# A graph attention block on one core: a fourth raw weight buffer, weights requested a slot sooner, and some steps put in another order

## The chip, the core and the metric

The kernel runs on one core of one Trainium2 chip. The metric is the device time of one execution in microseconds; for each kernel the median of several runs is given. The engines are called as in the profile: PE (matrix products; PEld is its weight load), DVE (vector), ACT (activations), POOL (GpSimd) and SP (the queue that issues most DMAs). Each engine works off its own queue in program order, and waits on semaphores for what other engines or DMAs must have done.

## What is computed

384 nodes with 1024 features, 6528 edges of five types, 16 heads of 64 features. All values are float32.

```python
h = relu(layernorm(x))                      # 384 x 1024
q, k, v = h @ wq.T + bq, h @ wk.T + bk, h @ wv.T + bv
q2, k2, v2 = q @ wiq.T + biq, k @ wik.T + bik, v @ wiv.T + biv      # then split in 16 heads
mask[src, dst] = softplus(edge_type_weights)[edge_type - 1]         # -inf where there is no edge
attn = softmax(q2 @ k2.T / 8 + mask)        # per head, 384 x 384
return x + (attn @ v2) @ wo.T + bo
```

When an edge occurs several times, the last one counts; the diagonal gets the fourth weight where no edge gives it one.

## The kernel before

To keep float32 accuracy on a product type that rounds its inputs, each operand is split in a high and a low half (`hi` is the rounded value, `lo` the rest), and each product is made three times: hi by hi, hi by lo, lo by hi (`mm3`, L366; lines L367, L368 and L369).

The seven weight matrices come as 56 chunks of 128x1024 (L51 to L55), in the order v, q, iv, k, then iq and ik in turn, then o. `load(w)` (L60) requests chunk w on SP into one of the `raw` buffers; `split_hi(w)` (L67) rounds it on ACT (L77), `split_lo(w)` (L79) subtracts on DVE or POOL (L82). The halves lie in four `whl` buffers. A chunk of a projection takes one "slot" of 24 products over 384 tokens. `slot_head(w)` (L395) opens a slot: it splits chunk w+2, evacuates the previous slot's bank, and calls load(w+4).

**Start** (L93 to L124, L311 to L363). SP requests the three tiles of x; between the first and the second stands the request of the edge rows `er` (L98). Then come chunk 0, the edges `ed`, chunk 1 and small constants. `key_rows` (L180) makes on POOL, in L182 to L184, a key of each edge from `er` and writes it to DRAM (`krow`); `key_load` (L196) reads it back, spread over all partitions, into `rows`. Then, for each x tile, DVE takes the statistics (L251, L254), ACT and POOL subtract the mean (L280, L282; DVE does so for tile 2), PE transposes (L292), `ln_hi` (L298) makes the high half on ACT and `ln_lo` (L303) the low one on DVE. POOL also splits chunk 0 (L344, L346), turns the edges into floats (L150) and makes the low half of chunk 1 (L82). `warm(n)` gives PE n idle transposes. The first chunk's 24 products (L410 to L415) have an order of their own: all eight hi by hi, then the others in groups of four.

**Projections.** Beside them, DVE looks for double edges (`mask_detect`, L217) in `rows`, and POOL scatters the mask values (L228) into three DRAM tables, which table_clear (L146) fills first from a tile `zero`. `evac_row` (L380) evacuates a bank through a tile of the tag `e` (L382, then ACT L383). The tiles `er`, `zero`, `kr` (the keys) and `lnt` (the statistics) have the tag `e` too, and that tag has EB buffers, used in turn.

**Attention** (L685 on). 48 steps (16 heads by three row tiles) run as a hand-written pipeline, L767 on. In round i: scores of step i on PE (`do_S`, L694, two products, two score banks); for i-1 `do_ttr` on DVE (L700: adds the mask, finds the extreme, writes an `e` tile and so frees the score bank); for i-2 the exponential on ACT (L704); for i-3 the normalisation (L708 on DVE, L709 on POOL); for i-5 the transposes on PE (`do_T`, L714); for i-6 their split (L723 on ACT, L724 on DVE); every third round the product with v2 (L731) and its evacuation (L741, L742, L746, L747). `fill(n)` puts other products between: first those of iq and ik (`fill_qk`, with `qk_head`, L576; `qk_done`, L548, evacuates with L377 and L378 and sends the halves through DMAs L557 to L567 to the stacks that the scores read), then those of the output matrix (`fill_o`, L657). `wo_prep` (L623) splits an output chunk and calls load(WO+k+2); OPOOL names the output chunks whose low half POOL makes.

**Output.** The output is summed in two halves of four chunks. After the fourth chunk `ysum` (L651, DVE's L654) adds the bank to the residual tile, and the bank becomes free for the next tile.

Of the kernel before, what the change touches and what calls it, by code (L numbers as in the profile page):

```python
# [8 lines left out]
F32 = mybir.dt.float32  # L9
# [5 lines left out]
N, D, NT, KT, NP = 384, 1024, 3, 8, 8  # L15
# [7 lines left out]
def gnn_kernel(ctx: ExitStack, tc: tile.TileContext, x, edges, erows, etw, wq, wk, wv, wiq, wik, wiv, wo,  # L23
# [6 lines left out]
    nc = tc.nc  # L30
    const = ctx.enter_context(tc.tile_pool(name="const", bufs=1))
    big = ctx.enter_context(tc.tile_pool(name="big", bufs=1))
    wpool = ctx.enter_context(tc.tile_pool(name="wpool", bufs=4))
# [2 lines left out]
    dram = ctx.enter_context(tc.tile_pool(name="dram", bufs=1, space=bass.MemoryType.DRAM))  # L36
    ctx.enter_context(tc.manual_schedule())

    EB = 8
    NTAB, RNG = 3, EC // 3  # L40
    JI = [0, 1, 3, 5, 8, 11, 14, RNG]
    WARM = (20, 6, 0)
# [1 line left out]
    def bank(tag):  # L44
        return psum.tile([128, 512], F32, tag=tag, name=tag, bufs={"g": 3, "a": 1}.get(tag, 2))
# [11 lines left out]
    raw, whl = {}, {}  # L57
    NCH = len(chunks)

    def load(w):  # L60
        if w >= NCH:
            return
        n, m = chunks[w]
        raw[w] = wpool.tile([128, D], F32, tag="raw", name="raw", bufs=3)
        nc.sync.dma_start(raw[w], W[n][m])

    def split_hi(w, dst=None, dve=False):  # L67
# [26 lines left out]
    er = ert[:, :2 * EC].bitcast(I32)  # L94
    for t in range(NT):
        nc.sync.dma_start(xt[t], x[t * 128:(t + 1) * 128, :])
        if t == 0:
            nc.sync.dma_start(er, erows)  # L98
    load(0)
    ed = const.tile([128, 3 * EC], I32, name="ed")  # L100
    nc.sync.dma_start(ed, edges)
# [78 lines left out]
    def key_rows():  # L180

        nc.gpsimd.tensor_copy(kf, er)  # L182
        nc.gpsimd.tensor_scalar(kf[:, :EC], kf[:, :EC], float(N), None, op0=OP.mult)
        nc.gpsimd.tensor_tensor(krt[:, :EC], kf[:, :EC], kf[:, EC:], OP.add)  # L184
        nc.sync.dma_start(krow.rearrange("c j -> (c j)").rearrange("(p e) -> p e", p=128), krt[:, :EC])
# [10 lines left out]
    def key_load(g, s):  # L196

        if s == 0:
            t = work.tile([128, 2, NT, N], F32R, tag="pt", name="rows")
            krv[g] = t.bitcast(F32).rearrange("p a k n -> p (a k n)")  # L200
        c0, c1 = parts(g)[s]
        dst = krv[g][:, s * PA * 128:(s * PA + c1 - c0) * 128]
        for c in range(c0, c1):
            rows[c] = krv[g][:, (s * PA + c - c0) * 128:(s * PA + c - c0 + 1) * 128]
        nc.sync.dma_start(dst, krow[c0:c1, :].rearrange("c j -> (c j)").partition_broadcast(128))
# [44 lines left out]
    def ln_bn(t, h):  # L250
        nc.vector.bn_stats(lnt[:, 30 + 12 * t + 6 * h:36 + 12 * t + 6 * h], xt[t][:, h * 512:(h + 1) * 512])  # L251
# [25 lines left out]
    def ln_sub(t, c0, c1, eng):  # L277
        src, dst = xt[t][:, c0:c1], xn[t][:, c0:c1]
        if eng is nc.scalar:
            nc.scalar.activation(dst, src, AF.Identity, bias=negm[:, t:t + 1])  # L280
        elif eng is nc.gpsimd:
            nc.gpsimd.tensor_tensor(dst, src, lnt[:, 2 * t:2 * t + 1].to_broadcast([128, c1 - c0]), OP.subtract)  # L282
        else:
            nc.vector.tensor_scalar(dst, src, lnt[:, 2 * t:2 * t + 1], None, op0=OP.subtract)
# [11 lines left out]
    def ln_hi(t, half, ps):  # L296
        hi = hT[:, 0, half * 4:half * 4 + 4, t * 128:(t + 1) * 128]
        nc.scalar.activation(hi, ps.rearrange("p (k n) -> p k n", k=4), AF.Relu)  # L298
# [11 lines left out]

    mask_consts()  # L311
    warm(WARM[0])
    key_rows()
    load(2)
    for s in range(NTAB):
        key_load(0, s)
    ln_bn(0, 0)
    ln_bn(0, 1)
    ln_mean(0)
# [1 line left out]
    ln_sub(0, 512, D, nc.gpsimd)  # L321
    p0 = ln_transpose(0)
    warm(WARM[1])
    ln_hi(0, 0, p0[0])
    ln_hi(0, 1, p0[1])
    ln_bn(1, 0)
    ln_bn(1, 1)
    ln_mean(1)
    ln_sub(1, 0, 512, nc.scalar)
    ln_sub(1, 512, D, nc.gpsimd)  # L330
    ln_bn(2, 0)
    ln_bn(2, 1)
    ln_mean(2)
# [10 lines left out]
        nc.gpsimd.tensor_copy(t0[:, 0, c], raw[0][:, c])  # L344
    for c in (slice(0, 512), slice(512, D)):
        nc.gpsimd.tensor_tensor(t0[:, 1, c], raw[0][:, c], t0[:, 0, c].bitcast(F32), OP.subtract)  # L346
    load(3)
    ln_hi(2, 0, p2[0])
    ln_hi(2, 1, p2[1])
    ln_root()  # L350
# [35 lines left out]
    w = 0  # L386
# [8 lines left out]
    def slot_head(w):  # L395
        if w > 0:
            split_hi(w + 2)
        if w != 1:
            flush()
        split_lo(w + 2)  # L400
        while post:
            post.pop(0)()
        load(w + 4)

    def proj(src, dst, bidx, extra=None):
        nonlocal w
        for m in range(8):
            slot_head(w)
            ps = bank("g")
            if w == 0:  # L410
                for a, b, ks in ((0, 0, range(KT)), (1, 0, range(4)), (0, 1, range(4)), (1, 0, range(4, KT)),
                                 (0, 1, range(4, KT))):
                    for k in ks:
                        nc.tensor.matmul(ps[:, :N], whl[0][a][:, k * 128:(k + 1) * 128], src[:, b, k, :],  # L414
                                         start=(a == b == k == 0), stop=(b == 1 and k == KT - 1))  # L415
            else:
                for k in range(KT):
                    colmm(ps, w, src, k)
                    if w == 1 and k == 3:
                        ln_row()  # L420
                        flush()
            pend.append(lambda ps=ps, m=m: evac_row(ps, dst[:, 0, m, :], dst[:, 1, m, :],
                                                bc[:, bidx * 8 + m:bidx * 8 + m + 1]))
            if extra:
                extra(m)
            w += 1
# [149 lines left out]
    def qk_head(w):  # L576
        first = w - W0 < 3
        if not first:
            load(w + 4)
            split_hi(w + 2)  # L580
        if pendq:
            pendq.pop(0)()
        if 0 < w - W0 < NTAB:
            mask_select(w - W0)
        if first:
            split_hi(w + 2)
        split_lo(w + 2, nc.gpsimd if (w + 2) % 2 == PAR else None)
        if first:
            load(w + 4)
        if w == W0:  # L590
            mask_select(0)

# [18 lines left out]
    WO = NCH - 8  # L611
# [1 line left out]
    LT, LA = 5, 7  # L613
    PRE, RATE, RATE_O, RATE_E = 84, 7.9, 8, 8
    WSTEPS = (37, 40, 42, 44, 47, 51)
    PAR, OPOOL, ODVE = 1, (2, 3, 6), (2,)

    otile = {}
    oacc = {}
# [3 lines left out]
    def wo_prep(k):  # L623

        dst = None
        if k == 4:
            otile[0] = gtile("g3").rearrange("p a k n -> p (a k n)")
        if 4 <= k < 7:
            g, b = otile[0], (k - 4) * 2048
            dst = (g[:, b:b + 1024], g[:, b + 1024:b + 2048])  # L630
        split(WO + k, nc.gpsimd if k in OPOOL else None, dst, k in ODVE)
        load(WO + k + 2)

    def xb_load():

# [15 lines left out]
    def ysum(a, c=(0, 512)):  # L651
        t, h = OT[a]
        y = xb[t][:, h * 512 + c[0]:h * 512 + c[1]]
        nc.vector.tensor_tensor(y, oacc[t, h][:, c[0]:c[1]], y, OP.add)  # L654
        return y

    def fill_o():  # L657


        first = [(0, 0), (0, 1), (1, 0), (1, 1), (2, 0), (2, 1)]  # L660
        first += [(a, k) for k in (2, 3) for a in range(3)] + [(a, k) for a in range(3, 6) for k in range(KH)]
        for a, k in first:
            while now[0] < wready[k] or now[0] < 6 * k + OREADY or (k == KH - 1 and now[0] < XSTEP + 3):
                yield 0
            if k == 0:
                oacc[OT[a]] = bank("g")
            omm(*OT[a], k)
            if k == KH - 1:
                ysum(a)
            yield 4  # L670
        bank_step = (0, 0, 0, 49, 50)
        todo = [(a, k) for k in range(KH, 7) for a in range(5)]
        while todo:
            ready = [q for q in todo if now[0] >= max(6 * q[1] + OREADY, wready[q[1]], bank_step[q[0]])]
            if not ready:
                yield 0
                continue
            a, k = ready[0]
            todo.remove(ready[0])
            if k == KH:  # L680
                oacc[OT[a]] = bank("gggss"[a])
            omm(*OT[a], k)
            yield 4
# [83 lines left out]
    for i in range(S + LA + 4):  # L767
        now[0] = i
        r = RATE if len(gens) == 2 else RATE_O if i < S else RATE_E
        fill(r / 2)  # L770
        if i < S:
            do_S(i)
        fill(r / 2)
        if 0 <= i - 1 < S:
            do_ttr(i - 1)
        if 0 <= i - 2 < S:
            do_exp(i - 2)
        if 0 <= i - 3 < S:
            do_norm(i - 3)
        if 0 <= i - LT < S:  # L780
            do_T(i - LT)
        j = i - LA
        if j >= 2 and (j - 2) % 3 == 0 and (j - 2) // 3 < 16:
            do_A((j - 2) // 3)
        if 0 <= i - LT - 1 < S:
            do_pt(i - LT - 1)
        if j >= 3 and (j - 3) % 3 == 0 and (j - 3) // 3 < 16:
            do_ao((j - 3) // 3)
        if j >= 4 and (j - 4) % 6 == 3:
            do_aos((j - 4) // 3)  # L790
        run_tasks()
        if i == XSTEP:
            assert len(gens) < 2
            xb_load()
        if i in WSTEPS:
            wo_prep(wp)
            wready[wp] = i + 2
            wp += 1
# [57 lines left out]
```

## Time and profile before

| | |
|---|---|
| runs: median (lowest to highest) | 302.63 us (301.64 to 302.9), 3 runs |
| the profiled execution | 302.19 us, span of its trace 300.5 us |
| granted clock of PE | 0.999 of full speed |
| busy share of the span: DVE, ACT, POOL | 67%, 52%, 52% |
| bytes moved | 55.12 MB, 183 GB/s over the span |
| first real product (L414) starts | 12.26 us |
| last step of the attention pipeline on DVE (L742) starts | 287.14 us |

The profile is one execution. Its page lists the busy time of the engines, the chain of work that ended last (followed back from the last instruction, at each step to what released it), and groups of instructions by line. The timeline lists instructions in order: start in us, duration in us, engine, line, operation, output<-input, shapes, count; in square brackets the engine's idle time before it and what ended it. PE's products overlap, so their durations are longer than their spacing: what counts is the distance from start to start.

The stretches of the run, with the busy time of each engine (and the number of instructions):

```profile
core 0: us, PE busy (x) PEld busy (x) DVE busy (x) ACT busy (x) POOL busy (x), PEclk, DMA share, GB/s
0.00:12.26 12.26, 8.71 (x51) 6.86 (x51) 6.55 (x14) 6.16 (x12) 7.25 (x19) 1.00 0.79 270
12.26:111.00 98.74, 98.74 (x527) 93.19 (x528) 70.08 (x191) 41.23 (x52) 60.42 (x66) 1.00 0.65 216
...
160.00:250.00 90.00, 89.93 (x545) 87.42 (x544) 59.27 (x173) 63.62 (x148) 48.86 (x47) 1.00 0.67 166
250.00:275.00 25.00, 24.77 (x134) 21.02 (x133) 19.24 (x55) 17.53 (x41) 18.20 (x16) 1.00 0.53 179
275.00:300.50 25.50, 21.98 (x117) 18.76 (x115) 10.55 (x18) 5.40 (x11) 4.12 (x5) 0.99 0.17 62
```

### The profile page before, as it was taken

The page shows a single profiled execution, that of the slowest core. Times are in us where ns is not written, and L with a number is a line of the kernel's source. Part 1 is how long each engine was busy: PE and PEld are TensorE (multiplying, and loading weights), DVE is VectorE, ACT ScalarE, POOL GpSimd, SP SyncE. Part 2 cuts the span into 40 slices and gives each one's busy share as a digit, 9 for nine tenths or more (in the row PEclk, how much of TensorE's full clock was granted, in tenths as well). Part 3 has the DMA queues.
Part 4 walks back from the last instruction along what each step waited for, and adds up shares of the span by engine and source line. Part 5 has one row for each costly group of instructions (what it writes and reads, how often), then busy time and mean ns, then how long its engine had stood idle before and what let it go on. Part 6 is the DMA issues. An engine that isn't in the chain of part 4 may idle for free.

```text
span 300.5 us, 4961 instructions
## 1 busy us (share of the span) xinstructions
PE 293.1 (98%) x1649; PEld 276.1 (92%) x1649; DVE 200.5 (67%) x492; ACT 154.9 (52%) x289; POOL 155.7 (52%) x164
## 2 busy tenths in 40 slices
PE   7899999999999999999999999999999999999995
PEld 5699999999988889999999999999999998888884
DVE  2959986655956463788865576767576757696523
ACT  3874644333422213554325667777777767676310
POOL 5865766271555785730033737373746467566210
PEclk9999999999999999999999999999999999999999
DMA  7899754642686668475369997646565636910005
GB/s 233 284 297 381 281 164 171 228 143 70 217 238 224 193 217 242 142 274 198 115 169 244 217 221 173 166 127 180 155 170 139 174 81 174 381 41 0 2 0 209
DMA packets 22377, 55.12 MB, mean 183 GB/s; under 512 B 4816, under 2 KB 8400, under 8 KB 22352
## 3 DMA queue, kind: packets, MB, share of 16 engines
q1 hardware_dynamic: 19968, 52.42, 57.7%
q0 software_dynamic: 2064, 1.80, 2.0%
q10 hardware_dynamic: 320, 0.59, 0.8%
q8 instruction: 13, 0.21, 0.3%
q14 instruction: 12, 0.10, 0.1%
HBM read 40.39 MB, written 4.97 MB: 151 GB/s over the span
## 4 chain that ended last, share of the span: by engine, by line
PE 95%; DMA 2%; DVE 1%; ACT 0%; issue 0%; SPq 0%
PE g L369 21%; PE g L367 21%; PE g L368 21%; PE s L694 6%; PE a L731 6%; PE t L714 5%; PE s L369 2%; PE s L368 2%; PE s L367 2%; DMA g<-in_x_dram 2%; PE t L369 2%; PE t L367 2%; PE t L368 2%; PE g L414 1%; PE a L369 1%; PE a L367 1%
## 5 line engine op out<-in xcount | busy, mean ns | idle before, releaser
L367 PE MATMUL g<-g,whl 128*128 128x384 f32 x312 | 106.4, 341 | 0.0
L369 PE MATMUL g<-g,whl 128*128 128x384 f32 x312 | 104.5, 335 | 0.0
L368 PE MATMUL g<-g,whl 128*128 128x384 f32 x312 | 104.2, 334 | 0.0
L228 POOL DMA_INDIRECT tab<-val,idx x51 | 57.6, 1129 | 40.3 <-issue 11.3
L77 ACT ACTIVATE whl<-raw 128x1024 fp32r<-128x1024 f32 x51 | 53.4, 1051 | 31.7 <-PE g L369 20.1
L709 POOL TENSOR_TENSOR e<-e,s 128x384 f32<-128x384 f32 x48 | 39.2, 830 | 41.2 <-DVE s L708 32.9
L368 PEld LDWEIGHTS g<-g,whl 128*128 128x128 f32 x312 | 58.7, 188 | 0.0
L367 PEld LDWEIGHTS g<-g,whl 128*128 128x128 f32 x312 | 58.6, 188 | 0.0
L369 PEld LDWEIGHTS g<-g,whl 128*128 128x128 f32 x312 | 58.5, 188 | 0.0
L82 DVE TENSOR_TENSOR whl<-raw,whl 128x1024 fp32r<-128x1024 f32 x41 | 50.2, 1224 | 9.6 <-ACT whl L77 7.9
L82 POOL TENSOR_TENSOR whl<-raw,whl 128x1024 fp32r<-128x1024 f32 x11 | 26.5, 2412 | 35.6 <-ACT whl L77 31.8
L383 ACT ACTIVATE g<-f,bc 128x384 fp32r<-128x384 f32 x24 | 14.8, 618 | 53.1 <-DVE f L382 46.8
L704 ACT ACTIVATE e<-e,s 128x384 f32<-128x384 f32 x48 | 29.4, 612 | 13.0 <-DVE s L700 13.0
L724 DVE TENSOR_TENSOR pt<-t,pt 128x384 fp32r<-128x384 f32 x48 | 26.4, 550 | 13.9 <-ACT pt L723 13.3
L723 ACT ACTIVATE pt<-t 128x384 fp32r<-128x384 f32 x48 | 23.2, 484 | 13.9 <-PE t L714 13.3
L700 DVE CUSTOM_DVE_ANT_0 e<-s,ma 128x384 f32<-128x384 f32 x48 | 26.3, 550 | 2.0 <-PE s L694 1.8
L694 PE MATMUL s<-ks,qs 128*128 128x384 f32 x96 | 25.3, 344 | 0.3 <-DVE s L700 0.2
L714 PE MATMUL t<-ident,e 128*128 128x128 f32 x144 | 23.5, 271 | 0.0
L382 DVE TENSOR_TENSOR f<-g,rrow 128x384 f32<-128x384 f32 x24 | 13.3, 555 | 13.5 <-PE g L369 7.6
L714 PEld LDWEIGHTS t<-ident,e 128*128 128x128 f32 x144 | 18.8, 140 | 3.1
L378 DVE SCALAR_TENSOR_TENSOR nat<-g,bc,nat 128x384 fp32r<-128x384 f32 x16 | 9.9, 618 | 16.4 <-ACT nat L377 14.4
L731 PE MATMUL a<-pt,vhl 128*128 128x384 f32 x96 | 20.8, 351 | 0.0
(147 smaller groups left out, 414.8 us busy)
## 6 DMA issues: line engine op xcount, KB each, us to landing
ks<-nat SPq DMA_DIRECT2D x30, 192.0 KB
raw<-in_wv_dram SPq DMA_DIRECT2D x8, 512.0 KB
raw<-in_wq_dram SPq DMA_DIRECT2D x8, 512.0 KB
raw<-in_wiv_dram SPq DMA_DIRECT2D x8, 512.0 KB
raw<-in_wk_dram SPq DMA_DIRECT2D x8, 512.0 KB
raw<-in_wiq_dram SPq DMA_DIRECT2D x8, 512.0 KB
raw<-in_wik_dram SPq DMA_DIRECT2D x8, 512.0 KB
raw<-in_wo_dram SPq DMA_DIRECT2D x8, 512.0 KB
```

The source lines that it names most:

```text
L77: nc.scalar.activation(dst[0], raw[w], AF.Copy)
L82: (eng or nc.vector).tensor_tensor(lo, raw[w], hi.bitcast(F32), OP.subtract)
L228: nc.gpsimd.indirect_dma_start(out=tabs[c // RNG], out_offset=bass.IndirectOffsetOnAxis(ap=idx[:, c:c + 1], axis=0), in_=val[:, c:c + 1], ...
L367: nc.tensor.matmul(ps, lhi, rhi, start=first, stop=False)
L368: nc.tensor.matmul(ps, lhi, rlo, start=False, stop=False)
L369: nc.tensor.matmul(ps, llo, rhi, start=False, stop=last)
L694: nc.tensor.matmul(ps[:, :N], qs[:, o, t * 128:(t + 1) * 128], ks[:, o, s, :], start=(s == 0), stop=(s == 1))
L704: nc.scalar.activation(es[i], es[i], AF.Exp, bias=s[:, 0:1], scale=-1.0, accum_out=s[:, 1:2])
L709: nc.gpsimd.tensor_tensor(es[i], es[i], s[:, 2:3].to_broadcast([128, N]), OP.mult)
L714: nc.tensor.transpose(ps[:, k * 128:(k + 1) * 128], es[i][:, k * 128:(k + 1) * 128], ident)
L724: nc.vector.tensor_tensor(lo, pv, hi.bitcast(F32), OP.subtract)
L731: nc.tensor.matmul(ps[:, :N], vhl[:, k, p, 2 * o:2 * o + 2, :], pts[h][:, s, k, :], start=(k == 0 and s == 0), stop=(k == 2 and s == 1))
```

## The change

- `raw` has four buffers instead of three, and every call of load asks for one chunk further: load(w+5) for load(w+4), load(WO+k+3) for load(WO+k+2). At the start load(3) stands beside load(2), and load(4) where load(3) was.
- The tag `e` has six buffers instead of eight.
- The edge rows are requested behind the third x tile instead of behind the first.
- `key_rows`, load(2) and the first `key_load`s stand behind the mean subtraction of x tile 1. On POOL the key rows so come after the second L282 instead of ahead of the first. The `ln_hi` of tile 0 stand behind the subtraction of tile 1 on ACT.
- The eight hi by hi products of chunk 0 are made for tokens 0 to 255 first and then for tokens 256 to 383, as sixteen. The others are as before.
- A sum of the output half (`ysum`) is put in a list. The list is worked off after the next `do_ttr`, or ahead of the next use of a bank.
- OPOOL gets chunk 4: its low half goes from DVE to POOL.

In the built order of instructions PE's queue differs in the sixteen products alone; DVE's in round 42 (the low half of output chunk 4 is gone, L700 stands ahead of two L654 instead of behind them); ACT's and POOL's in what is named above.

```diff
-    EB = 8
+    EB = 6
...
-        raw[w] = wpool.tile([128, D], F32, tag="raw", name="raw", bufs=3)
+        raw[w] = wpool.tile([128, D], F32, tag="raw", name="raw", bufs=4)
...
         nc.sync.dma_start(xt[t], x[t * 128:(t + 1) * 128, :])
-        if t == 0:
-            nc.sync.dma_start(er, erows)
+    nc.sync.dma_start(er, erows)
...
     warm(WARM[0])
-    key_rows()
-    load(2)
-    for s in range(NTAB):
-        key_load(0, s)
     ln_bn(0, 0)
...
     warm(WARM[1])
-    ln_hi(0, 0, p0[0])
-    ln_hi(0, 1, p0[1])
     ln_bn(1, 0)
     ln_bn(1, 1)
     ln_mean(1)
     ln_sub(1, 0, 512, nc.scalar)
     ln_sub(1, 512, D, nc.gpsimd)
+    ln_hi(0, 0, p0[0])
+    ln_hi(0, 1, p0[1])
+    key_rows()
+    load(2)
+    load(3)
+    for s in range(NTAB):
+        key_load(0, s)
...
-    load(3)
+    load(4)
...
-        load(w + 4)
+        load(w + 5)
...
-                for a, b, ks in ((0, 0, range(KT)), (1, 0, range(4)), (0, 1, range(4)), (1, 0, range(4, KT)),
-                                 (0, 1, range(4, KT))):
+                al = (0, N)
+                for a, b, ks, (n0, n1) in ((0, 0, range(KT), (0, 256)), (0, 0, range(KT), (256, N)),
+                                           (1, 0, range(4), al), (0, 1, range(4), al), (1, 0, range(4, KT), al),
+                                           (0, 1, range(4, KT), al)):
...
-            load(w + 4)
+            load(w + 5)
...
-    PAR, OPOOL, ODVE = 1, (2, 3, 6), (2,)
+    PAR, OPOOL, ODVE = 1, (2, 3, 4, 6), (2,)
...
-        load(WO + k + 2)
+        load(WO + k + 3)
...
+    ysums = []
+
+    def flush_y():
+        while ysums:
+            ysum(ysums.pop(0))
...
             if k == 0:
+                flush_y()
                 oacc[OT[a]] = bank("g")
             omm(*OT[a], k)
             if k == KH - 1:
-                ysum(a)
+                ysums.append(a)
...
             do_ttr(i - 1)
+        flush_y()
```

More of the change, by code (lines that the diff above doesn't have):

```diff
@@ L410, in proj @@
             if w == 0:
-                for a, b, ks in ((0, 0, range(KT)), (1, 0, range(4)), (0, 1, range(4)), (1, 0, range(4, KT)),
-                                 (0, 1, range(4, KT))):
+                al = (0, N)
+                for a, b, ks, (n0, n1) in ((0, 0, range(KT), (0, 256)), (0, 0, range(KT), (256, N)),
+                                           (1, 0, range(4), al), (0, 1, range(4), al), (1, 0, range(4, KT), al),
+                                           (0, 1, range(4, KT), al)):
                     for k in ks:
-                        nc.tensor.matmul(ps[:, :N], whl[0][a][:, k * 128:(k + 1) * 128], src[:, b, k, :],
-                                         start=(a == b == k == 0), stop=(b == 1 and k == KT - 1))
+                        nc.tensor.matmul(ps[:, n0:n1], whl[0][a][:, k * 128:(k + 1) * 128], src[:, b, k, n0:n1],
+                                         start=(a == b == k == n0 == 0), stop=(b == 1 and k == KT - 1))
             else:
@@ L588, in qk_head @@
         if first:
-            load(w + 4)
+            load(w + 5)
         if w == W0:
@@ L775, in gnn_kernel @@
             do_ttr(i - 1)
+        flush_y()
         if 0 <= i - 2 < S:
```

## The prediction

> **What bounds the kernel now.** I read the page first (parts 1 and 4), then the chain in order of time for the start, then timelines of the few places where the matrix engine stands still. The page says that there is little to win:
>
> ```profile
> PE 293.1 (98%) x1649; PEld 276.1 (92%) x1649; DVE 200.5 (67%) x492; ACT 154.9 (52%) x289; POOL 155.7 (52%) x164
> PE 95%; DMA 2%; DVE 1%; ACT 0%; issue 0%; SPq 0%
> ```
>
> 95% of the chain that ended last is matrix products. A matrix product over 384 columns starts every 0.173 us, one over 512 every 0.227, and from 12.26 to 160 us PE is busy without a gap. What is not products lies in three places: the first 12.26 us, a few waits of L694 between 160 and 270, and the 3.5 us after the last product (297.0 to 300.5), which no edit touches. The start, by the chain in order of time:
>
> ```profile
> 1.72 5.41 DMA g<-in_x_dram
> 7.16 1.30 DVE lnt L251 x2
> ...
> 11.51 0.66 PE a L292 x4
> 12.17 0.09 issue
> ```
>
> The second x tile (landed 7.13) sets everything up to the first product. But POOL has a chain of its own beside it:
>
> ```profile
> 4.35 0.27 POOL L182 CAST er<-er 128x102 f32<-128x102 int32 x1 [1.77 <-DMA er<-in_erows_dram]
> ...
> 5.20 0.29 POOL L184 TENSOR_TENSOR kr<-er 128x51 f32<-128x51 f32 x1
> ...
> 8.77 1.04 POOL L282 TENSOR_TENSOR g<-g,lnt 128x512 f32<-128x512 f32 x1 [1.96 <-DVE lnt L254]
> 9.81 1.36 POOL L344 CAST whl<-raw 128x512 fp32r<-128x512 f32 x2
> 11.14 2.72 POOL L346 TENSOR_TENSOR whl<-raw,whl 128x512 fp32r<-128x512 f32 x2
> 13.79 0.33 POOL L150 CAST ed<-ed 128x153 f32<-128x153 int32 x1
> 14.20 2.41 POOL L82 TENSOR_TENSOR whl<-raw,whl 128x1024 fp32r<-128x1024 f32 x1
> ```
>
> From 8.77 it has no gap, and it ends at 16.61 with the low half of chunk 1's weights. The first product that reads them, L369 of chunk 1, starts at 16.85 with no gap before it. So PE and POOL arrive together: POOL's slack is about 0.15 us. That is the row to remember.
>
> The waits in attention:
>
> ```profile
> 162.35 1.06 ACT L77 ACTIVATE whl<-raw 128x1024 fp32r<-128x1024 f32 x1 [2.26 <-DMA raw<-in_wiq_dram]
> ...
> 166.19 0.62 PE L694 MATMUL s<-ks,qs 128*128 128x384 f32 x2
> ```
> ```profile
> 260.91 1.49 DVE L654 TENSOR_TENSOR g<-g,g 128x512 f32<-128x512 f32 x2
> 262.31 0.55 DVE L700 CUSTOM_DVE_ANT_0 e<-s,ma 128x384 f32<-128x384 f32 x1
> ...
> 262.92 0.62 PE L694 MATMUL s<-ks,qs 128*128 128x384 f32 x2 [0.23 <-DVE s L700]
> ```
>
> An undisturbed pair of L694 takes 0.51, a held one 0.57 to 0.62, plus the gap before it. Start to start against the undisturbed spacing, the held pairs lose 0.25 (at 166.19), 0.31 (172.08), 0.22 (192.6), 0.22 (207.4), 0.50 (262.92) and 0.26 (265.24): 1.76 us in all.
>
> **The change part by part.**
>
> *Fourth raw buffer, request a slot sooner.* load(w+4) with three buffers waits for the buffer of chunk w+1; load(w+5) with four waits for the same buffer. So no new wait stands in SP's queue, and each weight tile arrives a slot (4.1 us) earlier. From 18.8 to 160 us no product waits, so there it gives 0. At 162.35 ACT waited 2.26 us for a tile requested at 157.67. Behind it in ACT's queue stood the evacuation L377 and the exponentials, behind those DVE's L378, the stack transfers L567 (issued 164.56) and the scores that read them. The held pairs at 166.19 and 172.08 come from that; a slot is more than the 2.26 us missing. Gain 0.25 + 0.31 = 0.56; bounds 0 (the next wait is DVE's own backlog there) and 0.56. The pairs at 192.6 and 207.4 stand behind DVE's L378 and L82, not behind a transfer: they stay.
>
> *Output sums put off.* At 259.4 DVE has finished L724, but takes L82 (1.23) and two L654 (1.49) before the L700 that frees the score bank. In the built order L700 comes first and L82 is gone from DVE, so L700 can start near 259.4 instead of 262.31, and the 0.50 goes. The pair at 265.24 waits for the next L700, behind the third L654, whose place doesn't change; with 1.23 us less ahead of it on DVE it just about makes it. I take 0.7 of 0.76; bounds 0.3 and 0.76.
>
> *The fourth output chunk's low half on POOL.* 2.40 us there (row of 255.64) for 1.23 on DVE. POOL is idle from 259.6 to 263.11, and L77 gives it the high half at 259.73: it ends near 262.1, about when the next L709 gets its reciprocal. Cost 0; if the cover fails, L709 is late by up to 2.4, and the transpose two steps later has about 2 of it to spare. [...]
>
> *Six softmax tiles.* L700 of step i takes the tile of step i-6. The transposes of i-6 stand in PE's queue ahead of the scores of i, for which L700 waits anyway: cost 0. In the projections the fourth product tile of L382 takes the zero tile, which the third table clear must have left. By the landings in the trace that was at 30.3; it comes one weight tile later, near 32, while L382 ran at 32.39; its bank is wanted at 37.5. Cost 0, cover 4 to 5 us.
>
> *Edge rows behind x.* The issue of x tile 1 moves from 1.72 to about 1.25, so it lands some 0.45 sooner, near 6.7. Bounds: 0.15 (51 KB at the 357 GB/s of the window 5 to 10) and 1.1 (if the small rows stall the engines for longer than their bytes). DVE, ACT and PE follow: transposes done near 11.7.
>
> *Key rows moved.* L182 to L184 leave an idle stretch of POOL (4.35 to 5.49, 1.14 us) and enter the gapless chain between L282 and L344. So the chain ends at 16.61 + 1.14 - 0.45 = 17.3, and L369 of chunk 1 starts near 17.35 instead of 16.85: **+0.5**. With x sooner by 0.15 it is +0.8, with 1.1 it is 0; below 0 hardly, since L344 needs the first weight tile, landed at about 9.8 before, with as many bytes ahead of it now. SP's queue: the key rows' write, now near 10.5 instead of 5.5, holds back chunks 2 and 3 (second and third in line) and the row loads. Chunk 2 lands near 13.7 instead of 12.8 and is split from 14 on; chunk 3 lands near 15 instead of 20.9, since it overtakes the rows; the rows end near 21.5 instead of 19.6, and L217 first wants them at 23.6. All covered.
>
> *ln_hi of tile 0 behind the subtraction of tile 1 on ACT.* Two times 0.6, now between 9.2 and 10.3; ln_hi of tile 1 would be possible at 10.0: 0.3 later, and still ahead of the transposes of tile 2 (11.7). Cost 0.
>
> *First products by tokens.* Eight over 384 become eight over 256 and eight over 128. The transposes of tile 2 stay ahead of them in PE's queue, so they don't start before 11.7. 256 columns cost 0.120 (row of 294.06). 128 columns with these weights are not in the trace. Nearest are the transposes over 128, 0.109 apart when warm, 0.213 in the first 5 us. [...] I take the row: +0.44. At 0.213 it is +1.27. PE's own path then ends chunk 0 at 11.8 + 0.08 + 1.83 + 16 x 0.173 = 16.5 (17.3 at the upper price), and reaches L369 at 16.85 (17.7). POOL's 17.35 ends later, so the +0.44 hides behind the +0.5; at the upper price the start costs +0.8 in all.
>
> **Sum.** The profiled execution took 302.19 (span 300.5, 1.69 around it): 302.19 + 0.5 - 0.56 - 0.7 = 301.4. The median of the runs is 302.63, 0.44 above it, so 301.9 on the scale of the median.
>
> **The rivals.**
> *A, the forecast:* start +0.5, stalls -1.26: 301.9. Chance 0.48.
> *B, the start is free:* x comes 1.1 sooner, POOL's chain ends where it did, all 1.3 are won: 302.63 - 1.3 = 301.3, with the held pairs at 192.6 and 207.4 gone too 300.9. For it: packets of x were slow just after the edge rows (first landing to last over 3 us). Against it: the bytes are few. Chance 0.2.
> *C, stalls only move:* DVE is 77% busy at 250 to 275, so the next L654 or L724 holds the next pair: start +0.5 to +0.8 and nothing back, 303.1 to 303.4. Chance 0.17.
> *D, slower: POOL's chain.* Place: L182 waits for the edge rows, now fourth in the queue, and L344, L346 and L82 stand behind it. Price: one for one on the first L369 of chunk 1. Before, its weights' low half ended at 16.61. From 18.1 on (16.76 + 1.3) the change is slower than before, from 19.6 on by over 0.5%. It takes edge rows that land after 10.1, or after 11.6; I expect 8.5. With that, 303.5 to 305. Chance 0.15.
>
> **The numbers.** A measurement of this kernel can tell about 0.5% (1.5 us) from no change: 301.1 to 304.1 counts as the same. A lies inside but for 0.05; of B 0.15 is below; C is inside but for 0.02; D is above with 0.12. Faster 0.2, same 0.66, slower 0.14. The range runs from B's lower figure to the foot of D, 300.8 to 303.7, and leaves out less than 0.2.
>
> **What would show it.** In the new profile: x tile 1 lands near 6.7; L182 stands between L282 and L344, and L82 on POOL ends near 17.3; the first L369 of chunk 1 follows with a gap; products over 128 columns 0.11 apart (or 0.2); no wait of ACT's L77 for a transfer near 160; L694 without waits near 166, 172, 263. It is wrong if the first L369 of chunk 1 starts before 16.9 or after 18, if rows or table clears hold L382 so long that a product waits before 50 us, or if the held pairs turn up elsewhere.

## The result and the profile after

| | before | after |
|---|---|---|
| median of the runs (lowest to highest) | 302.63 us (301.35 to 303.27), 9 runs | 301.01 us (300.39 to 301.45), 9 runs |
| ratio to before, 95% interval | | 0.9952 (0.9936 to 0.9969) |
| the profiled execution / its span | 302.19 / 300.5 us | 301.08 / 299.4 us |

The forecast was 301.9 us, -0.24%, with a range of 300.8 to 303.7 (-0.6% to +0.35%). Measured is 301.01 us; the ratio makes it -0.48%, and the two medians -0.54% (the ratio follows the means of the runs, here and below). The gain is small but clear of the noise. It is twice the forecast's, and the range holds it with 0.2 us to spare. The page of the changed kernel looks almost as before:

```profile
PE 292.4 (98%) x1657; PEld 276.7 (92%) x1657; DVE 199.5 (67%) x491; ACT 155.0 (52%) x289; POOL 159.9 (53%) x165
PE 95%; DMA 2%; DVE 1%; SPq 0%; issue 0%
```

Three distances on PE's timeline divide the run, and all kernels below are told in them. "Start" ends where the first score product (the L694 of the kernel before) begins. "Middle" reaches from there to the first score product of step 41. "Tail" is the rest of the span.

| us | first real product | start ends | middle | tail |
|---|---|---|---|---|
| before | 12.26 | 160.85 | 95.79 | 43.85 |
| after | 11.69 | 160.74 | 95.22 | 43.42 |
| difference | -0.57 | -0.11 | -0.57 | -0.43 |

The differences of the three stretches add up to 1.11, and 302.19 - 1.11 is the 301.08 of the profiled execution. Each line of the table is one execution; how far others stray is told with the experiments.

**The start.** In the changed kernel some lines have moved: L250 and L281 are the former L251 and L282, L181 to L183 are the key rows, L416 is the first chunk, L704 the scores, L710 the mask step of `do_ttr`, L656 the output sum. The chain in order of time (start, duration, what) now comes from tile 2, not from tile 1:

```profile
1.73 6.34 DMA g<-in_x_dram
8.09 1.30 DVE lnt L250 x2
...
11.93 4.62 PE g L416 x32
```

x tile 1 landed at 5.40 (7.14 before), tile 2 at 8.06 (8.49 before), the edge rows at 8.27 (4.30 before). So DVE has done tile 1 when tile 2 comes, and tile 2 sets the first product. POOL, the engine that the forecast feared, in its timeline of the same kernel:

```profile
7.18 1.04 POOL L281 TENSOR_TENSOR g<-g,lnt 128x512 f32<-128x512 f32 x1 [0.34 <-DVE lnt L253]
8.32 0.27 POOL L181 CAST er<-er 128x102 f32<-128x102 int32 x1
...
9.57 1.36 POOL L344 CAST whl<-raw 128x512 fp32r<-128x512 f32 x2
...
13.96 2.41 POOL L82 TENSOR_TENSOR whl<-raw,whl 128x1024 fp32r<-128x1024 f32 x1
```

The key rows (8.32 to 9.47) fill a hole: the first weight tile lands at 9.52, and L344 could not have begun before. POOL's chain ends at 16.37, 0.24 sooner than before. PE does not feel it, as its own timeline shows:

```profile
11.69 4.87 PE L416 MATMUL g<-g,whl 128*128 128x256 f32 x32
...
16.74 0.33 PE L369 MATMUL g<-g,whl 128*128 128x384 f32 x1
```

The first L369 of chunk 1 follows its neighbours at the usual 0.17. Of the 0.57 that PE starts sooner, 0.46 goes to the narrow products (from the first product to the first score product it is 149.05 us, 148.59 before), and 0.11 is left.

**The middle.** ACT's timeline: the weight split that waited 2.26 us for its transfer begins at once, and the next wait is one for PE.

```profile
159.26 1.05 ACT L77 ACTIVATE whl<-raw 128x1024 fp32r<-128x1024 f32 x1
162.32 0.58 ACT L377 ACTIVATE nat<-g,bc 128x384 fp32r<-128x384 f32 x1 [2.02 <-PE g L369]
```

The score pairs near 166 and 172 take 0.51, undisturbed; those at 191.6 and 206.4 stay held, 0.22 each.

**The tail.** DVE's and PE's timelines of the round with the output sums:

```profile
258.60 0.55 DVE L710 CUSTOM_DVE_ANT_0 e<-s,ma 128x384 f32<-128x384 f32 x1
...
262.85 0.69 DVE L656 TENSOR_TENSOR g<-g,g 128x512 f32<-128x512 f32 x1
263.46 0.55 DVE L710 CUSTOM_DVE_ANT_0 e<-s,ma 128x384 f32<-128x384 f32 x1
```
```profile
261.84 0.52 PE L704 MATMUL s<-ks,qs 128*128 128x384 f32 x2
...
264.07 0.61 PE L704 MATMUL s<-ks,qs 128*128 128x384 f32 x2
```

The L710 ahead of the first pair now starts at 258.60 instead of 262.31, and the pair at 261.84 is free. The next L710 still stands behind the third sum (262.85), and the pair at 264.07 loses 0.25, as the one at 265.24 did before: its two products come 0.38 and 0.28 after their neighbours, 0.23 and 0.17 when undisturbed.

### The profile page after: what moved, and what is told of

It is laid out like the page before. It is cut to its first block, busy times and chain, and to the rows that moved or that the text cites. A ratio compares the mean times of both kernels' runs of the same rounds, so it can differ in the third digit from the quotient of the medians.

```text
span 299.4 us, 4984 instructions
## 1 busy us (share of the span) xinstructions
PE 292.4 (98%) x1657; PEld 276.7 (92%) x1657; DVE 199.5 (67%) x491; ACT 155.0 (52%) x289; POOL 159.9 (53%) x165
## 4 chain that ended last, share of the span: by engine, by line
PE 95%; DMA 2%; DVE 1%; SPq 0%; issue 0%
PE g L369 22%; PE g L367 21%; PE g L368 21%; PE s L704 6%; PE a L741 6%; PE t L724 5%; DMA g<-in_x_dram 2%; PE s L368 2%; PE s L367 2%; PE s L369 2%; PE g L416 2%; PE t L369 2%; PE t L367 2%; PE t L368 2%; PE a L369 1%; PE a L367 1%
## 5 line engine op out<-in xcount | busy, mean ns | idle before, releaser
L369 PE MATMUL g<-g,whl 128*128 128x384 f32 x312 | 104.5, 335 | 0.0
L227 POOL DMA_INDIRECT tab<-val,idx x51 | 58.6, 1150 | 37.4 <-DMA tab<-val,idx 11.9
L77 ACT ACTIVATE whl<-raw 128x1024 fp32r<-128x1024 f32 x51 | 53.5, 1051 | 27.9 <-PE g L369 21.1
L719 POOL TENSOR_TENSOR e<-e,s 128x384 f32<-128x384 f32 x48 | 39.2, 829 | 38.4 <-DVE s L718 30.0
L369 PEld LDWEIGHTS g<-g,whl 128*128 128x128 f32 x312 | 58.5, 188 | 0.0
L82 DVE TENSOR_TENSOR whl<-raw,whl 128x1024 fp32r<-128x1024 f32 x41 | 50.1, 1222 | 11.8 <-ACT whl L77 11.8
L82 POOL TENSOR_TENSOR whl<-raw,whl 128x1024 fp32r<-128x1024 f32 x11 | 26.5, 2408 | 35.8 <-ACT whl L77 32.1
L710 DVE CUSTOM_DVE_ANT_0 e<-s,ma 128x384 f32<-128x384 f32 x48 | 26.3, 549 | 3.4 <-PE s L704 3.3
L704 PE MATMUL s<-ks,qs 128*128 128x384 f32 x96 | 25.0, 341 | 0.0
L382 DVE TENSOR_TENSOR f<-g,rrow 128x384 f32<-128x384 f32 x24 | 13.3, 555 | 14.8 <-PE g L369 14.6
```

Source lines behind the costliest of these rows:

```text
L77: nc.scalar.activation(dst[0], raw[w], AF.Copy)
L82: (eng or nc.vector).tensor_tensor(lo, raw[w], hi.bitcast(F32), OP.subtract)
L227: nc.gpsimd.indirect_dma_start(out=tabs[c // RNG], out_offset=bass.IndirectOffsetOnAxis(ap=idx[:, c:c + 1], axis=0), in_=val[:, c:c + 1], ...
L369: nc.tensor.matmul(ps, llo, rhi, start=False, stop=last)
L704: nc.tensor.matmul(ps[:, :N], qs[:, o, t * 128:(t + 1) * 128], ks[:, o, s, :], start=(s == 0), stop=(s == 1))
L719: nc.gpsimd.tensor_tensor(es[i], es[i], s[:, 2:3].to_broadcast([128, N]), OP.mult)
```

## The experiments

Theory: three independent terms, -0.1 from the start, -0.57 from the loads, -0.43 from sums and POOL. Rivals: the terms need each other; the start's freedom is only luck of the landings; one of two edits in the tail does all the work. Each kernel was timed in five rounds against the kernel before on the same chip; before had a median of 302.38, 302.59 and 302.81 in the three batches (23 to 33 runs each, 301.4 to 304.8). "Start", "middle" and "tail" are from one profile of each. The diffs are cut down to what is named.

### The start alone

Before with the edits of the start: edge rows behind x, key rows and ln_hi moved, sixteen narrow first products.

```diff
-        if t == 0:
-            nc.sync.dma_start(er, erows)
+    nc.sync.dma_start(er, erows)
...
-    key_rows()
-    load(2)
...
     ln_sub(1, 512, D, nc.gpsimd)
+    ln_hi(0, 0, p0[0])
+    ln_hi(0, 1, p0[1])
+    key_rows()
+    load(2)
...
```

> The kernel before with the edits of the start alone: edge rows behind x, key rows and the first row loads behind the subtraction of tile 1, products of chunk 0 by tokens. Raw buffers, load positions, softmax tiles and output sums as before. Theory 1 (the change's gain comes from waits in attention, the start gives 0.1 us because the split products and POOL's chain eat what the earlier x tile gives): 0.0 to -0.3 us against before. Theory 2 (the profiled pair hides it, and the start gives most of the 1.6 us between the medians): -0.8 to -1.2 us. In its trace x tile 1 lands near 5.4 by both.

302.14 us, ratio 0.9984 (0.9965 to 1.0003). The first product begins at 11.10, 1.16 sooner than before, yet the start ends at 160.75, only 0.10 sooner. The narrow products take 0.46 of it. About 0.25 goes at chunk 1, whose L82 on POOL ends at 16.24: the first product reading it starts at 16.29, 0.31 after its neighbour, and the next 0.28 after that, instead of 0.17 each. The remaining 0.3 goes behind 24.57; ACT's, DVE's and PE's timelines (in this kernel L366 is the first product of a group):

```profile
22.10 1.06 ACT L77 ACTIVATE whl<-raw 128x1024 fp32r<-128x1024 f32 x1 [2.06 <-DMA raw<-in_wv_dram]
```
```profile
23.20 1.23 DVE L82 TENSOR_TENSOR whl<-raw,whl 128x1024 fp32r<-128x1024 f32 x1 [4.27 <-ACT whl L77]
24.34 0.55 DVE L381 TENSOR_TENSOR f<-g,rrow 128x384 f32<-128x384 f32 x1
```
```profile
24.57 0.34 PE L368 MATMUL g<-g,whl 128*128 128x384 f32 x1
24.95 0.44 PE L366 MATMUL g<-g,whl 128*128 128x384 f32 x1
```

With three buffers, chunk 3 is still requested behind the row loads, and these now go out later. ACT waits for it, DVE's L82 waits for ACT, and L381, which evacuates the bank that PE wants next, stands behind L82 and ends at 24.89. The product at 24.95 starts 0.38 after its neighbour, the one after it 0.28.

The middle of this profile is 95.24, nearly that of the changed kernel, though this kernel has three buffers and ACT waits for the transfer as before:

```profile
161.68 1.06 ACT L77 ACTIVATE whl<-raw 128x1024 fp32r<-128x1024 f32 x1 [1.99 <-DMA raw<-in_wiq_dram]
```

No pair near 166 or 172 is held. The five profiles with three buffers have middles of 95.79 (before), 95.77, 95.94, 95.56 and 95.24. In the four with a held pair this L77 begins 1.29 to 1.77 us after the first score product, here 0.93. So the held pairs of the middle depend on when the tile lands in an execution, and the term of the loads is 0.44 on the average of these five, not 0.57 each time.

### The loads alone

Before with four raw buffers, six softmax tiles and every request a slot sooner.

```diff
-    EB = 8
+    EB = 6
...
-        raw[w] = wpool.tile([128, D], F32, tag="raw", name="raw", bufs=3)
+        raw[w] = wpool.tile([128, D], F32, tag="raw", name="raw", bufs=4)
...
-            load(w + 4)
+            load(w + 5)
...
```

> The kernel before with four raw buffers, six softmax tiles and every chunk requested a slot sooner, nothing else. Theory 1: the transfer wait of ACT near 162 us goes and with it the two held score pairs at 166.2 and 172.1, 0.56 us; -0.5 to -0.6 us in the profile, and up to -1.0 in the median if that wait is longer in other executions. Theory 2: 0 to -0.3 us. A rival for the gain: if six softmax tiles held anything, a wait of L700 or L382 that is not in the trace of before would show.

302.14 us, ratio 0.9992 (0.9972 to 1.0012): by the runs alone nothing could be said. In the profile ACT has no wait:

```profile
160.12 1.05 ACT L77 ACTIVATE whl<-raw 128x1024 fp32r<-128x1024 f32 x1
```

The pairs near 166 and 172 are free, and the middle is 95.22, exactly as in the changed kernel (95.79 before). Eight profiles with four buffers have these pairs free; the ninth is told with the last versions. The start of that execution was late (first product at 12.73), which hides the 0.57 in its time.

### Sums and POOL alone

Before with the list of output sums and chunk 4 in OPOOL.

```diff
-    PAR, OPOOL, ODVE = 1, (2, 3, 6), (2,)
+    PAR, OPOOL, ODVE = 1, (2, 3, 4, 6), (2,)
...
-                ysum(a)
+                ysums.append(a)
...
             do_ttr(i - 1)
+        flush_y()
...
```

> The kernel before with the output sums put off and the low half of output chunk 4 on POOL, nothing else. Theory 1: the held score pair at 262.9 goes, the one at 265.2 stays: -0.5 us. Theory 2: 0 to -0.2 us.

302.0 us, ratio 0.9991 (0.9967 to 1.0014). Tail 43.38 (43.85 before), middle 95.77, with ACT's wait for the transfer still there (3.07 us at 162.53). So loads and sums touch different stretches, and neither takes from the other.

### Wide first products

The changed kernel with the eight wide products of before.

```diff
-                for a, b, ks, (n0, n1) in ((0, 0, range(KT), (0, 256)), (0, 0, range(KT), (256, N)),
-                                           (1, 0, range(4), al), (0, 1, range(4), al), (1, 0, range(4, KT), al),
-                                           (0, 1, range(4, KT), al)):
+                for a, b, ks in ((0, 0, range(KT)), (1, 0, range(4)), (0, 1, range(4)), (1, 0, range(4, KT)),
+                                 (0, 1, range(4, KT))):
...
```

> The changed kernel with the eight first products over 384 tokens again. The sixteen narrow ones cost 1.87 us for 1.39. Theory 1: the products then start near 11.95 instead of 11.69, since they need tile 2's high half, and chunk 0 ends near 16.1 instead of 16.4; POOL's low half of chunk 1 (ready at 16.4) then sets L369, which starts near 16.5: -0.2 us against the changed kernel. Theory 2 (the early start is worth more than the narrow products cost): +0.2 us or more.

301.39 us (300.66 to 301.57), ratio 0.9945 (0.9924 to 0.9967); the changed kernel has 0.9952. The two intervals overlap nearly whole: it tells nothing either way. Nor does the profile, whose first product begins at 12.66: in that execution the transposes ahead of it were 0.21 us apart until 10.9, and in the changed kernel's 0.11 from 7 on.

### The changed kernel again

No edit; it stands in the second batch as a measure for the next three.

> The changed kernel itself, beside the next three on one chip, so that they have something to be compared with. 0.4 to 0.6% below before again by every theory.

301.09 us, ratio 0.9947 (0.9923 to 0.997). Middle 95.22 and tail 43.41, as in the first profile.

### Edge rows behind tile 0 again

The changed kernel, with that one request where it was before.

```diff
     for t in range(NT):
         nc.sync.dma_start(xt[t], x[t * 128:(t + 1) * 128, :])
-    nc.sync.dma_start(er, erows)
+        if t == 0:
+            nc.sync.dma_start(er, erows)
```

> The changed kernel with the edge rows requested behind x tile 0 again, all else as changed. Theory 1 (the place of the small rows decides when x tile 1 lands): tile 1 lands at 7.1 instead of 5.4, POOL's L281 of tile 1 ends at 9.8, the key rows at 10.9, so chunk 0's split runs 1.35 later and the low half of chunk 1 is ready at 17.7: L369 of chunk 1 near 17.8, +1.0 to +1.2 us against the changed kernel. Rival (tile 1 comes early because of its own earlier request alone, or by chance of an execution): +0.3 us or less.

302.29 us, ratio 0.9974 (0.9955 to 0.9993): 1.2 us above the changed kernel of the same batch, and its lowest run is above the highest of that one's eight (301.36). Middle and tail are unchanged (95.22, 43.39). In its profile tile 1 landed at 8.06, and POOL did what rival D and the forecast feared:

```profile
9.70 1.04 POOL L282 TENSOR_TENSOR g<-g,lnt 128x512 f32<-128x512 f32 x1 [2.76 <-DVE lnt L254]
10.68 0.27 POOL L182 CAST er<-er 128x102 f32<-128x102 int32 x1
...
15.94 2.41 POOL L82 TENSOR_TENSOR whl<-raw,whl 128x1024 fp32r<-128x1024 f32 x1
```
```profile
18.41 0.44 PE L370 MATMUL g<-g,whl 128*128 128x384 f32 x1 [0.34 <-POOL whl L82]
```

From 9.70 POOL has no gap, the key rows' 1.2 us lie in the chain, and PE waits for its end. That wait costs 0.61: this product comes 0.68 after its neighbour and the next 0.28 after it, instead of 0.17 each. The first product, at 12.71, is late by 1.0 besides. The mechanism exists. It needs POOL's subtraction for the x tile to end less than the key rows' 1.2 us ahead of the landing of the first weights, or behind it: here it ended at 10.74 and they landed at 10.63; in the changed kernel it is 8.22 and 9.52.

### Start and loads without the sums

Both edits together on before (the two diffs above).

> The kernel before with the edits of the start, four raw buffers, earlier requests and six softmax tiles: the whole change but the output sums and the moved low half. Alone the start gave 0.24 us and the loads 0.24 us between medians. Theory 3 (they need each other: with the key rows late, chunk 3 behind the row loads comes so late that a product waits for a bank near 24.6 us, 0.3 us, and the earlier requests take that wait away): -0.8 to -1.0 us against before, more than the sum of both. Rival (the parts add up): -0.5 us.

301.58 us, ratio 0.996 (0.9943 to 0.9978), 1.0 us below before, against 0.24 for each alone by the medians. That is not clear of a plain sum: the two ratios alone multiply to 0.9976, inside the interval. What the profile shows is that the 0.31 us stall behind 24.57 is gone: products follow there at 0.17 without a gap. The fourth buffer lets the later rows cost nothing, since chunk 3 is requested ahead of them. In this place the edits need each other, and a forecast that adds them one by one misses that.

### The sums alone

Only the list of sums on before; chunk 4's low half stays on DVE.

```diff
-                ysum(a)
+                ysums.append(a)
...
             do_ttr(i - 1)
+        flush_y()
...
```

> The kernel before with the output sums put off alone (the low half of output chunk 4 stays on DVE). Theory 1 (either of the two is enough for the held pair at 262.9): L700 follows L82 at 261.0 instead of the two sums at 262.3, before PE wants the bank at 262.5: the 0.50 goes, as with both. Rival (both are needed): half of it stays.

303.2 us, ratio 0.9999 (0.9977 to 1.0021). The tail is 43.70, 0.15 below before. The first pair is free, but the second is held for longer than it was:

```profile
264.55 0.52 PE L702 MATMUL s<-ks,qs 128*128 128x384 f32 x2
...
267.05 0.61 PE L702 MATMUL s<-ks,qs 128*128 128x384 f32 x2 [0.26 <-DVE s L708]
```

From the product ahead of it (266.39) to 267.05 it is 0.66 instead of the 0.23 of an undisturbed place. DVE's 1.23 us for the low half of chunk 4 have not gone away; they are late one round further on.

### POOL's low half alone

```diff
-    PAR, OPOOL, ODVE = 1, (2, 3, 6), (2,)
+    PAR, OPOOL, ODVE = 1, (2, 3, 4, 6), (2,)
```

> The kernel before with the low half of output chunk 4 on POOL alone (the sums stay ahead of L700). Theory 1: the sums start near 259.7 to 260.2 instead of 260.9 and L700 near 261.5, just ahead of PE at 262.5: the 0.50 goes. Rival (the second sum waits for its products, which end near 260.7, so L700 starts at 261.4 or later and part of the wait stays): 0.1 to 0.3 us stay.

302.58 us, ratio 0.9984 (0.9961 to 1.0008), tail 43.85: nothing. DVE's timeline and PE's:

```profile
262.13 0.69 DVE L654 TENSOR_TENSOR g<-g,g 128x512 f32<-128x512 f32 x1 [0.35 <-PE g L369]
262.74 0.55 DVE L700 CUSTOM_DVE_ANT_0 e<-s,ma 128x384 f32<-128x384 f32 x1
```
```profile
263.35 0.61 PE L694 MATMUL s<-ks,qs 128*128 128x384 f32 x2 [0.23 <-DVE s L700]
```

DVE is free sooner, but the second sum in its queue waits for its own products, and L700 stands behind that sum. Only both edits together free the pair: 0.15 and 0 alone, 0.47 together.

### What is left: a version meant to hold no score pair

The changed kernel, with one sum put behind the L710 that it stood ahead of, and with DVE's low halves of the iq and ik chunks put behind the next `do_ttr`. Their targets are the held pairs at 191.6, 206.4 and 264.07.

```diff
-        split_lo(w + 2, nc.gpsimd if (w + 2) % 2 == PAR else None)
+        if first or (w + 2) % 2 == PAR:
+            split_lo(w + 2, nc.gpsimd if (w + 2) % 2 == PAR else None)
+        else:
+            los.append(w + 2)
...
-    def flush_y():
-        while ysums:
+    def flush_y(n=0):
+        while len(ysums) > n:
...
-                flush_y()
+                flush_y(1)
                 oacc[OT[a]] = bank("g")
...
         flush_y()
+        while los:
+            split_lo(los.pop(0))
...
```

> The changed kernel with two steps more in the same manner: an output sum waits for the next L710 also where a bank is taken that it doesn't hold, and DVE's low halves of the iq and ik chunks are made behind the next L710 instead of ahead of it. Theory 1: the held score pairs at 191.6, 206.4 and 263.7 (0.22 + 0.22 + 0.31) go: -0.7 us against the changed kernel. Rival: the low halves come later, so the next chunk's buffer is freed later and its transfer or the exponentials hold something else: 0 or above.

300.3 us (300.04 to 300.63), ratio 0.9918 (0.9893 to 0.9943). PE's timeline has the third pair at

```profile
263.66 0.52 PE L708 MATMUL s<-ks,qs 128*128 128x384 f32 x2
```

without a hold; middle 94.85 (95.22) and tail 43.14 (43.42), 0.65 together. The runs differ from those of the changed kernel in the same batch by 0.79.

The same with wide first products:

> The kernel with the two steps more, and the eight first products over 384 tokens again. The sixteen narrow products take 0.46 us more of PE, but start without tile 2's high half. Alone the wider products gave +0.3 us with overlapping times. Theory 3 (the wide ones wait for ACT's L297 of tile 2, near 12.6 for the second four, and then for POOL's low half of chunk 1): +0.1 to +0.3 us against the next kernel. Rival (the narrow ones are a pure cost): -0.3 us.

300.55 us, ratio 0.9913 (0.9883 to 0.9943). Its first product starts at 11.51, later than the third tile's transposes by 0.75 instead of 0.41, since it must have all three tiles' high halves; the products of the chunk are then 0.46 shorter; and the first product that reads POOL's L82 (ended 16.29) starts at 16.35, 0.41 behind its neighbour instead of 0.17. What the split costs and what it saves are a few tenths each. Which is larger stays open: the intervals overlap. Its middle is 95.15, for the pair at 171.48 is held by 0.3 although this kernel has four buffers and ACT's L77 at 159.76 did not wait; what held it is not known.

The best version again, on the same chip as that:

> The kernel with the two steps more once again, beside the one above. 300.3 us by every theory, 0.7 below the changed kernel.

300.25 us (299.93 to 300.43), ratio 0.9907 (0.988 to 0.9935): the lowest median of all, about 0.8 us below the changed kernel's of the two earlier batches.

## Why the prediction was right, and where it was not

The number lies in the range, and the waits that it reckoned with in attention, ACT's near 162 and PE's at 262.9, are gone. The part on the start was wrong, by the forecast's own sign: the first L369 of chunk 1 begins at 16.74, ahead of the 16.9 that it had named as the limit. The measured 301.01 is nearer to rival B's 301.3 ("the start is free", chance 0.2) than to forecast A's 301.9, and it is in the range because the range was drawn from B's lower figure. That two errors of opposite sign, 0.6 and 0.27, cancel in part is luck.


- **Fourth buffer and requests.** Expected 0.56, measured 0.57 in the pair of profiles, and nothing before 160 by themselves. Right in mechanism; the size depends on the execution, since with three buffers the same pairs were once free (the start alone) and lost 0.34 to 0.72 in the other four. What the step did not see: together with the start they also take away a stall that the start alone makes behind 24.57.
- **Edge rows behind x: the size failed.** Expected 0.45 sooner, bounds 0.15 and 1.1; tile 1 came 1.74 sooner, outside the bounds. PE's first product then moved by only 0.57, because tile 2, whose landing moved by 0.43, took over. It is not the luck of one execution: tile 1 landed between 7.04 and 8.06 in the six profiles with the rows ahead of it, and between 5.32 and 5.68 in the eight with the rows behind x. The kernel with that one request put back cost 1.2 us.
- **Key rows moved: the step that failed.** "L182 to L184 ... enter the gapless chain between L282 and L344. So the chain ends at 16.61 + 1.14 - 0.45 = 17.3" counted +0.5; measured is 16.37, and no cost. The chain is gapless only as long as POOL's subtraction ends about when the first weights land, or later. With tile 1 at 5.40 the gate is the first weight tile (9.52), and the key rows stand in the wait for it. The forecast had named this floor ("L344 needs the first weight tile, landed at about 9.8") but used it only to exclude a gain. With the edge rows put back, the chain that was forecast appeared, and its price, 0.61, is near the 0.5 forecast.
- **Narrow first products.** 1.83 expected, 8 x (0.120 + 0.109) from the row of 256 columns and that of the transposes; 1.88 measured from the first of the sixteen to the product behind them. 128 columns are 0.111 apart, so the row of the transposes was the right one. But they were to hide behind POOL's chain, and as that chain was not late, they are on the path: they eat 0.46 of the 0.57.
- **Output sums: too large.** 0.7 of 0.76 expected, 0.43 measured. The pair at 262.9 is free, as reckoned. The second stays, because the third sum is ahead of its L710; "it just about makes it" was a hope, not a sum. The best version, with that sum moved, frees it.
- **POOL's low half.** Cost 0, as expected: L82 took 2.40 on POOL (259.12 to 261.52), no more than the one at 254.95, and DVE's sum beside it (259.97) took 0.69, no more than the one at 262.85. The next L719 at 261.94 waited for DVE's reciprocal, not for POOL. Another pair of the same profile was longer side by side: L757 on POOL took 2.00 (265.05; 1.01 to 1.02 in its seven other places) beside DVE's L82, 1.71 (264.46; the 41 into whl average 1.22). Why the one pair was and the other was not is not shown.
- **Six softmax tiles.** Cost 0: the fourth L382 was at 32.33, 32.39 before.

The net is the forecast's mechanism in two of three terms (1.0 of the 1.1 won is freed waits in middle and tail), with a start of -0.1 instead of +0.5 and sums of 0.43 instead of 0.7: 0.6 better, 0.27 worse. By that the median should be 302.63 - 1.11 = 301.5, 0.5 above the measured one. Other executions explain part of it. The start ends at 161.11 on the average of the four profiles at full clock that have the start of before (160.76 to 161.51), and at 160.74 in the five with the whole new start and four buffers (160.43 to 161.09): -0.37, not -0.11. With -0.44 for the loads and -0.43 for the tail this makes -1.24. The slower runs of before told in the last section may explain some more, and the rest is within the spread of the runs.

## What to carry to other kernels

A chain "without a gap" is so under its present gate only: before adding a step's cost to it, move the gate and look which arrival is next, here the first weights behind the x tile. When an engine's backlog holds a buffer, freeing time on that engine and moving the release ahead are two halves of one edit: here 0 and 0.15 us alone, 0.47 together. With gains of 0.2 to 0.5% per part, the spacing of the same products in two profiles tells what the medians can't. But a profile is one execution: a wait that hangs on a landing, like the one at 162.35, needs several before its size is known.

## What the hardware showed that was not expected

**A small transfer between large ones.** The edge rows are 51 KB in rows of 408 bytes. Their bytes are worth 0.15 us by the forecast's estimate and their issue puts off that of the next tile by 0.46 (1.72 against 1.26), but with them between two x tiles the next tile landed 1.74 us later (7.14 against 5.40 in the two profiles first compared). The landing varies from execution to execution, but the two orders do not overlap: 7.04 to 8.06 in six profiles, 5.32 to 5.68 in eight. The parts of the transfer show where it goes. In the first pair the sixteen parts of tile 1 land from 5.36 to 7.14 behind the rows, and from 4.95 to 5.40 without them: the first part is 0.41 later, near the 0.46 of the issue, and the last parts lag. Why they lag was not tried.

**Half clock for 3.41 us at the start.** In the profile of the kernel with the sums alone, PE's granted clock falls shortly before the first product (13.04). The stretches of that profile (from:to, length, busy time of PE, PEld, DVE, ACT, POOL, clock, DMA share, GB/s):

```profile
8.00:10.00 2.00, 0.63 (x6) 0.36 (x4) 1.97 (x5) 1.11 (x4) 0.49 (x1) 1.00 1.02 384
...
12.00:14.00 2.00, 2.00 (x9) 1.71 (x8) 2.00 (x5) 1.48 (x4) 2.00 (x2) 0.50 0.21 84
14.00:16.00 2.00, 2.00 (x10) 2.00 (x9) 1.89 (x5) 2.00 (x4) 1.43 (x3) 0.65 0.88 252
```

The record has half clock from 11.98 to 15.39, and the 24 products of chunk 0 took 5.34 us instead of 4.25. PE had stood idle for 1.84 us until 10.47, for x tile 1. This is one trace. It has the longest such gap of the fourteen; the next longest, 1.74 (POOL's low half alone) and 1.68 (the loads alone), left the clock at 1.00.

That execution took 304.07 us, at a mean granted clock of 0.994. Of 141 runs of kernels with the edge rows between the x tiles, 25 have such a mean, 0.992 to 0.994 instead of 0.997 to 1.0, and take 303.2 us or more; of 69 runs of kernels with the rows behind x, none. The changed kernel with that one request put back has it in 1 of 12. So the lower clock goes with the place of the rows, and a part of the change's gain is that it no longer occurs: without these runs the mean of before's 81 later runs falls from 302.77 to 302.47, the median from 302.45 to 302.38. That PE's wait for tile 1 is the cause is the author's guess; the gap was not tried alone.

**The transposes speed up at different times.** In all profiles PE's first transposes are 0.213 us apart and later ones 0.109. The change comes at 4.4 to 6.5 us in ten of the fourteen, and at 10.3 to 10.9 in four, whatever the kernel. Among the four is the one with wide first products; the same products in the last version, sped up early, began 1.15 us sooner (11.51). So the starts of two single profiles can differ by this alone. What sets the moment is not shown.
